# Two alternating running sums in place of one chain in the softmax sums of a graph-attention kernel

## Chip, cores, metric

One core of one Trainium2 chip runs the whole kernel. The metric is device time in microseconds (us), the median of several runs; lower is better. Engines are called as in the profile: PE is TensorE (matmuls), PEld its weight loads, DVE is VectorE, ACT is ScalarE, POOL is GpSimd, SP issues most DMAs.

## The reference, cut to what matters

Two layers on x of shape (16, 1024, 256), each with a layer norm and a relu ahead of it and a residual around it. Layer 0 builds a weight matrix per batch, from it the queries, and then runs softmax attention with four heads of 64 channels; layer 1 is a graph convolution with two linear layers and batch norms. What the change touches is the softmax:

```python
c_adj = jnp.mean(fea, axis=1)
diff = c_adj[:, None, :] - c_adj[:, :, None]
A = jnp.abs(jnp.abs(jax.nn.sigmoid(diff) - 0.5) - 0.5) * 2.0
...
Wg = adj[None, :, :] * A_s
g = jnp.einsum('bcn,bnm->bcm', fea, Wg)
...
attn = jax.nn.softmax(jnp.einsum('bhnd,bhmd->bhnm', q, k) * scale, axis=-1)
out = jnp.einsum('bhnm,bhmd->bhnd', attn, v)
```

## The kernel before, in words

Everything is fp32. The order of the work on every engine is written out by hand (a manual schedule): each engine executes its instructions in the order in which the Python code issues them, and only waits on semaphores are put in between. So "ahead" and "behind" below are places in an engine's queue.

**The loop.** One pass per batch b of 16. It runs the attention of batch b (`attention`, line 732), then the graph of batch b+1 (`graph` at line 385 for b+1 = 1, `graph_seven` at line 501 for the 14 batches from 2 to 15), then the first linear layer of batch b (`linear1_all`). After the loop an output stage does the second linear layer and the residual. A pass through the middle of the loop takes some 131 us.

**The attention** has four steps, two halves g of the queries times two pairs of heads. In a step, `scores` (line 737) loops over eight blocks m of 128 keys. For each, PE makes two 128x512 blocks of scores into one PSUM tile f_s (line 743, three buffers), ACT takes the exponential of the tile into an SBUF tile f_p (line 751, eight buffers), and DVE adds it to a running sum f_acc: block 1 to block 0 at line 757, blocks 2 to 7 into the sum in place at line 760. The sum over the eight tiles is still spread over 128 keys. `partial` (line 764) finishes it: a DVE transpose in 32x32 blocks from f_acc into f_sums (line 768; f_sums is in pool `ow`, one buffer) and a DVE reduction into f_red (line 776). `values` (line 778) multiplies the exponentials by v on PE (line 784) into one PSUM tile f_o, which DVE transposes into f_oT (line 797). PE does scores and values of a step one after the other, and goes on with the next step's scores.

**Between the steps** stand other pieces:
- `hooks` for steps 0 and 1, issued between `scores` and `partial`: `weights(b+1, c)` for c = 0 and 1. That is `differences` (line 350), two ACT operations that make a 128x1024 weight tile f_w from a row of means f_row (absolute value at line 353, tanh at line 356), and `masked` (line 359), one DVE operation that multiplies it by the adjacency tile (line 361). f_row comes by a DMA through DRAM. For b = 0 the hooks also hold column sums of the adjacency on ACT and two small DVE operations; for b = 15 only a relu on ACT.
- the reciprocal of the sums of half 0, in step 2: `collect` (line 807), four ACT copies from f_red to f_parts, is issued inside `scores` after block 5; `invert` (line 814), four DVE operations on f_rec, f_most and f_least (lines 817 to 820), and `spread`, four ACT copies to f_recs (line 826), stand between `scores` and `partial`; `scale` (line 835), one DVE multiplication of f_oT and 16 DMAs on SP, follows `partial`.

**The graph** of the next batch follows on PE right behind the last values. Eight weight tiles c of 128 rows go into it. Tiles 0 and 1 are used plainly (`plain`, matmuls at line 514); tiles 2 to 7 go in three pairs n through a scheme with seven products instead of eight. Its DVE work is a list written out from line 606 on: maskings of tiles 2 to 7 (line 361), the reciprocal of half 1 (lines 817 to 820), differences of halves of the tiles (`make_t1` to `make_t4`, lines 557 to 569, some of them in place in f_w), and the scaling of half 1 (line 835). The matmuls of the pairs are at line 576. PE's list near the end of the maskings is m1(1), m2(1), m4(0), m_7(1), m3(1), m1(2), m2(2), m6(0), m6(1); m1(2) reads tile 6 and m2(2) tile 7.

Of the kernel before, what the change touches and what calls it, by code (L numbers as in the profile page):

```python
# [10 lines left out]
F32 = mybir.dt.float32  # L11
# [6 lines left out]
P = 128  # L18
# [11 lines left out]
def fast_path(  # L30
# [20 lines left out]
    nc = tc.nc  # L51
# [48 lines left out]
    class BatchNorm:  # L100
# [11 lines left out]
        def invert(self, f0, f1, triples=None):  # L112
            for f in range(f0, f1):
                nc.vector.bn_aggr(
                    self.mv[:, f, :],
                    self.st[:, f, :, :].rearrange("p t s -> p (t s)")
                    if triples is None
                    else triples,
                )
            at = slice(f0, f1)  # L120
            nc.vector.tensor_scalar_add(self.var[:, at], self.mv[:, at, 1], EPS)
            nc.gpsimd.tensor_tensor(
                self.rstd[:, at], self.var[:, at], mhalf[:, : f1 - f0], ALU.pow
            )
            if self.offset is not None:
                mean = self.mv[:, at, 0]
                nc.vector.tensor_add(mean, mean, self.offset[:, at])
                nc.vector.tensor_sub(mean, self.offset[:, at], mean)
# [47 lines left out]
    with ExitStack() as stage:  # L176
# [5 lines left out]
        ow = stage.enter_context(tc.tile_pool(name="fow", bufs=1))  # L182
# [15 lines left out]
        for c in range(NC):  # L198
            if LASTING[c] is None:
                t = big.tile([P, N], F32, tag=f"adj{c}", name=f"f_adj_{c}")  # L200
            else:
                t = lasting.tile(
                    [P, N], F32, tag=LASTING[c], name=f"f_adj_{c}", bufs=4 if c < 4 else 1
                )
# [527 lines left out]
        def attention(b, qT, kT, v, hooks):  # L732

            steps = [(g, pair) for g in range(NH) for pair in range(HEADS // 2)]
            p_of, acc_of, oT_of, o_of, red_of = {}, {}, {}, {}, {}

            def scores(s, within=None):
                g, pair = steps[s]
                for m in range(NC):
                    ps = ps_s.tile([P, 2, 512], F32, tag="s", name=f"f_s_{b}_{s}_{m}")  # L740
                    for e in range(2):
                        rows_e = slice(e * HD, (e + 1) * HD)
                        nc.tensor.matmul(  # L743
                            ps[:, e, :],
                            kT[rows_e, pair, ts(m, P)],
                            qT[rows_e, pair, ts(g, 512)],
                            start=True,
                            stop=True,
                        )
                    p = pp.tile([P, 2, 512], F32, tag="p", name=f"f_p_{b}_{s}_{m}")  # L750
                    nc.scalar.activation(p, ps, AF.Exp)  # L751
                    p_of[s, m] = p
                    if m == 1:
                        acc = pp.tile(
                            [P, 2, 512], F32, tag="acc", name=f"f_acc_{b}_{s}", bufs=2
                        )
                        nc.vector.tensor_add(acc, p_of[s, 0], p)  # L757
                        acc_of[s] = acc
                    elif m > 1:
                        nc.vector.tensor_add(acc_of[s], acc_of[s], p)  # L760
                    if m == 5 and within:
                        within()

            def partial(s):

                g, pair = steps[s]
                t = ow.tile([P, 2, 16, 32], F32, tag="sums", name=f"f_sums_{b}_{s}")
                nc.vector.transpose(
                    t.rearrange("p e j i -> p (e j i)"),
                    acc_of.pop(s).rearrange("p e q -> p (e q)"),  # L770
                )
                if pair == 0:
                    red_of[g] = small.tile(
                        [P, HEADS // 2, 2, 16], F32, tag="red", name=f"f_red_{b}_{g}", bufs=1
                    )
                nc.vector.tensor_reduce(red_of[g][:, pair], t, AX.X, ALU.add)  # L776

            def values(s):
                g, pair = steps[s]
                o_of[s] = ps_o.tile([P, 512], F32, tag="o", name=f"f_o_{b}_{s}")  # L780
                for m in range(NC):
                    p = p_of.pop((s, m))
                    for e in range(2):
                        nc.tensor.matmul(  # L784
                            o_of[s][e * HD : (e + 1) * HD, :],
                            v[:, m, ts(2 * pair + e, HD)],
                            p[:, e, :],
                            start=(m == 0),
                            stop=(m == NC - 1),
                        )  # L790
                if pair == 0:
                    oT_of[g] = ow.tile(
                        [P, HEADS // 2, 4, 4, 32], F32, tag="oT", name=f"f_oT_{b}_{g}", bufs=2
                    )


                nc.vector.transpose(
                    oT_of[g][:, pair].rearrange("p j c i -> p c j i"),
                    o_of.pop(s).rearrange("p (c j i) -> p c j i", c=4, j=4),
                )  # L800
# [65 lines left out]
            first = finish(0)  # L866
            collect, invert, spread, scale, add = first
            for i in range(len(steps)):
                scores(i, collect if i == 2 else None)
                for step in hooks.get(i, ()):  # L870
                    step()
                if i == 2:
                    invert()
                    spread()
                partial(i)
                if i == 2:
                    scale()
                values(i)
# [419 lines left out]
        with tc.manual_schedule(engines={ENG.PE, ENG.Activation, ENG.DVE, ENG.Pool, ENG.SP}):  # L1298
# [73 lines left out]
            for b in range(B):  # L1372

                hooks = {}
# [7 lines left out]
                else:  # L1382
                    hooks[0] = [lambda norm=norm: norm.relu(4, NC, False)]
                    w2n = lasting.tile([P, CC, F1], F32, tag="w2n", name="f_w2n")
                    nc.sync.dma_start(w2n, W2.rearrange("(c p) f -> p c f", p=P))
                left = attention(b, *qkv, hooks)

                def more(c):
# [102 lines left out]
    with ExitStack() as stage:  # L1491
# [21 lines left out]
        with tc.manual_schedule(engines={ENG.PE, ENG.Activation, ENG.DVE, ENG.Pool, ENG.SP}):  # L1513
# [31 lines left out]
            sums = lasting.tile([P, 4, 2, P], F32, tag="w2n", name="f_w2s")  # L1545
# [825 lines left out]
```

## Time and profile before

| | |
|---|---|
| median of 3 runs | 2397.92 us (2396.44 to 2398.54) |
| profiled execution: span | 2396.9 us, in 24478 instructions |
| the span beside the median | 1.0 us shorter |
| granted PE clock, mean | 0.995 (1.00 until 2330 us, 0.83 in the last 67 us) |
| DVE adds at line 760 | 384, 470.5 us busy, 1225 ns each |
| DVE adds at line 757 | 64, 76.3 us busy, 1192 ns on the page |
| DVE maskings at line 361 | 127, 152.7 us busy, 1212 ns each |
| ACT exponentials at line 751 | 512, 477.4 us busy, 1048 ns each |
| PE scores, line 743, and values, line 784 | 457.1 and 453.6 us busy |

The page says how busy each engine is over the whole span. The timeline lists the instructions of one engine in order of time; neighbours of one kind are merged into a row with a count, and the first number is the start, the second the time from the first start to the last end. A remark in brackets gives the engine's idle time ahead of the row and what ended it. The records of DVE, ACT and PE instructions overlap their neighbours by some tens of ns[...]; so the distance from start to start tells what an instruction costs its queue, and the duration does not.

Busy time by stretch of one pass, PE, DVE and ACT: attention of batch 8 (1117 to 1175 us) 58.0, 55.3 and 42.4 of 58; the graph up to its last masking (1175 to 1191) 15.8, 15.8 and 9.8 of 16; the rest of the graph (1191 to 1219) 28.0, 22.6 and 11.0 of 28; the linear layer (1219 to 1250) 31.0, 20.4 and 10.9 of 31.

### The profile page before, as it was taken

The numbers are of one execution on the slowest core, as the hardware profiler recorded it, in microseconds if no ns is written. First come the engines' busy times: TensorE is split into PE (matmuls) and PEld (weight loads), VectorE is DVE, ScalarE is ACT, GpSimd is POOL, SyncE is SP. The second block draws the span as 40 slices with busy tenths as digits, with TensorE's granted clock in tenths as the row PEclk, the third lists the DMA queues.
The fourth block names the chain that finished last, engine by engine and source line by source line (L and its number), as shares of the span: only waits on it lengthen the run. The fifth ranks groups of instructions, "written<-read, shape, count | busy, mean of one in ns | idle before, by whom it ended". The sixth has DMA issues, their size and how long they took to land.

```text
span 2396.9 us, 24478 instructions
## 1 busy us (share of the span) xinstructions
PE 2353.8 (98%) x7950; PEld 1032.4 (43%) x7950; DVE 1974.2 (82%) x2806; ACT 1346.8 (56%) x1974; POOL 174.1 (7%) x253
## 2 busy tenths in 40 slices
PE   8999999999999999999999999999999999999995
PEld 4443444434343434444343434344443434444444
DVE  6888889797979798897979797988979798757766
ACT  6845555564736455555647374555555565346654
POOL 2030010101010000101010100001010100000000
PEclk9999999999999999999999999999999999999998
DMA  5042433433342434334323414243433321355569
GB/s 189 8 143 93 144 116 123 136 117 91 98 156 64 160 93 160 100 123 136 120 96 111 140 61 164 87 167 93 137 123 121 115 85 53 114 208 181 174 243 371
DMA packets 178650, 312.44 MB, mean 130 GB/s; under 512 B 33617, under 2 KB 117073, under 8 KB 178513
## 3 DMA queue, kind: packets, MB, share of 16 engines
q1 hardware_dynamic: 164176, 267.25, 33.2%
q0 software_dynamic: 9728, 26.76, 3.7%
q10 hardware_dynamic: 4608, 16.78, 1.7%
q8 instruction: 65, 1.06, 0.2%
q14 instruction: 73, 0.59, 0.1%
HBM read 195.04 MB, written 96.79 MB: 122 GB/s over the span
## 4 chain that ended last, share of the span: by engine, by line
PE 72%; DVE 18%; ACT 4%; issue 3%; DMA 1%; SPq 1%; DVEq 0%; ACTq 0%; POOLq 0%; POOL 0%
PE f_aps L944 16%; PE f_s L743 12%; PE f_o L784 11%; PE f_zps L1050 6%; DVE f_acc L760 6%; PE f_vps L450 5%; PE f_zx L1588 4%; DVE f_w L361 4%; PE f_gpsx L576 3%; PE f_zm L1588 3%; ACT f_p L751 3%; PE f_gps L576 3%; PE f_kpsx L691 2%; PE f_gps L404 2%; PE f_kps L691 2%
## 5 line engine op out<-in xcount | busy, mean ns | idle before, releaser
L751 ACT ACTIVATE f_p<-f_s 128x1024 f32<-128x1024 f32 x512 | 477.4, 1048 | 163.0 <-PE f_s L743 163.0
L760 DVE TENSOR_TENSOR f_acc<-f_acc,f_p 128x1024 f32<-128x1024 f32 x384 | 470.5, 1225 | 41.4 <-DVE f_acc L760 1.4
L743 PE MATMUL f_s<-f_qT,f_kT 64*128 64x512 f32 x2048 | 457.1, 596 | 0.0
L784 PE MATMUL f_o<-f_p,f_v 128*64 128x512 f32 x2048 | 453.6, 595 | 0.0
L743 PEld LDWEIGHTS f_s<-f_qT,f_kT 64*128 64x128 f32 x2048 | 190.2, 185 | 264.4 <-ACT f_p L751 118.6
L784 PEld LDWEIGHTS f_o<-f_p,f_v 128*64 128x64 f32 x2048 | 141.4, 137 | 304.4 <-issue 251.3
L353 ACT ACTIVATE f_w<-f_row,f_col 128x1024 f32<-128x1024 f32 x127 | 147.0, 1157 | 31.6 <-PE f_gps L514 16.8
L361 DVE SCALAR_TENSOR_TENSOR f_w<-f_w,f_adj 128x1024 f32<-128x1024 f32 x127 | 152.7, 1212 | 4.2 <-ACT f_w L356 4.2
L260 POOL TENSOR_TENSOR f_rstd_b<-f_var_b,f_mhalf 128x4 f32<-128x4 f32 (+1 forms) x31 | 33.1, 1069 | 1502.3 <-DVE f_var_b L259 1502.3
L356 ACT ACTIVATE f_w<-f_w 128x1024 f32<-128x1024 f32 x127 | 134.3, 1058 | 4.0
L944 PE MATMUL f_aps<-f_ahatT,f_hs 128*128 128x512 f32 x256 | 115.1, 592 | 0.0
L944 PE MATMUL f_aps<-f_ahatT,f_h_b 128*128 128x512 f32 x256 | 113.4, 596 | 0.0
L450 PE MATMUL f_vps<-f_kvw,f_hT 128*128 128x256 f32 x512 | 113.1, 379 | 0.0
L944 PE MATMUL f_aps<-f_t,f_hs 128*128 128x512 f32 x256 | 112.5, 592 | 0.0
L281 ACT ACTIVATE f_h_b<-f_x,f_shift_b,f_rstd_b 128x256 f32<-128x256 f32 x128 | 66.3, 593 | 75.7 <-DVE f_shift_b L266 75.7
L450 PEld LDWEIGHTS f_vps<-f_kvw,f_hT 128*128 128x128 f32 x512 | 97.3, 190 | 20.1 <-issue 7.4
L281 ACT ACTIVATE f_h_a<-f_x,f_shift_a,f_rstd_a 128x256 f32<-128x256 f32 x126 | 73.8, 587 | 50.5 <-DVE f_shift_a L266 50.5
L514 PE MATMUL f_gps<-f_w,f_h_a 128*128 128x512 f32 x224 | 99.9, 599 | 0.0
L757 DVE TENSOR_TENSOR f_acc<-f_p,f_p 128x1024 f32<-128x1024 f32 x64 | 76.3, 1192 | 14.4 <-ACT f_p L751 14.4
L576 PE MATMUL f_gps<-f_w,f_h_a 128*128 128x512 f32 x168 | 82.7, 601 | 3.8 <-DVE f_w L361 3.8
L1073 ACT ACTIVATE f_z<-f_zps,f_b 128x512 f32<-128x512 f32 x60 | 38.0, 683 | 75.3 <-PE f_zps L1050 75.3
L776 DVE TENSOR_REDUCE f_red<-f_sums 128x32 f32<-128x1024 f32 x64 | 78.1, 1220 | 2.2
(275 smaller groups left out, 3410.6 us busy)
## 6 DMA issues: line engine op xcount, KB each, us to landing
f_t<-ft SPq DMA_DIRECT2D x84, 512.0 KB, 10.9
fz<-f_z SPq DMA_DIRECT2D x64, 512.0 KB, 9.6
f_x<-in_x_dram SPq DMA_DIRECT2D x31, 1024.0 KB, 6.3
f_zb<-fz SPq DMA_DIRECT2D x42, 512.0 KB, 4.2
f_att<-f_oT SPq DMA_DIRECT2D x512, 32.0 KB, 1.9
fx<-f_x SPq DMA_DIRECT2D x16, 1024.0 KB, 4.4
fhT<-f_hQ POOLq DMA_DIRECT2D x112, 128.0 KB, 2.9
f_hT<-fhT SPq DMA_DIRECT2D x28, 512.0 KB, 6.0
```

Source lines behind the costliest of these rows:

```text
L281: nc.scalar.activation(self.h[:, c, :], self.xt[:, c, :], AF.Relu, bias=self.shift[:, c : c + 1], scale=self.rstd[:, c : c + 1], accum_out ...
L353: nc.scalar.activation(w, rows[b], AF.Abs, bias=cols[b][:, c : c + 1], scale=0.5 / C)
L361: nc.vector.scalar_tensor_tensor(w, w, 1.0, adj_t[c], ALU.subtract, ALU.mult)
L450: nc.tensor.matmul(ps[:, i, :], hT[e][:, ts(c4 + i, P)], kvw_t[:, e, C : 2 * C], start=(e == 0), stop=(e == CC - 1),)
L576: nc.tensor.matmul(ps, left, right, start=fresh and n == 0, stop=(n == PAIRS - 1), skip_group_check=more,)
L743: nc.tensor.matmul(ps[:, e, :], kT[rows_e, pair, ts(m, P)], qT[rows_e, pair, ts(g, 512)], start=True, stop=True,)
L751: nc.scalar.activation(p, ps, AF.Exp)
L760: nc.vector.tensor_add(acc_of[s], acc_of[s], p)
L784: nc.tensor.matmul(o_of[s][e * HD : (e + 1) * HD, :], v[:, m, ts(2 * pair + e, HD)], p[:, e, :], start=(m == 0), stop=(m == NC - 1),)
L944: nc.tensor.matmul(ps, left[:, m, :], right(m), start=not more and m == 0, stop=(m == KH - 1), skip_group_check=more,)
L1050: nc.tensor.matmul(ps[i], left[:, ts(i, P)], right, start=not more, stop=True, skip_group_check=more,)
L1588: nc.tensor.matmul(ps, left[:, m, :], right[:, m, :], start=start and m == 0, stop=(m == 1), skip_group_check=not start,)
```

## The change

The running sum is split. Block 1 still starts f_acc from blocks 0 and 1. Block 2 is not added alone any more: at block 3, a second sum starts in the f_sums tile, from blocks 2 and 3. From then on even blocks (4 and 6) are added to f_acc, odd blocks (5 and 7) to f_sums. One more add joins f_sums into f_acc; there are seven adds in a step, as before. The join is issued at the end of `scores`, behind the steps that used to stand between `scores` and `partial`: the hooks (with the weight tile's masking) and, in step 2, `invert` and `spread`. The transpose in `partial` then writes into the same f_sums tile that held the second sum, so that tile is taken at block 3 of a step and not at its end.

```diff
-            p_of, acc_of, oT_of, o_of, red_of = {}, {}, {}, {}, {}
-
-            def scores(s, within=None):
+            p_of, acc_of, odd_of, oT_of, o_of, red_of = {}, {}, {}, {}, {}, {}
+
+            def scores(s, within=None, before_last=()):
...
                         acc_of[s] = acc
-                    elif m > 1:
-                        nc.vector.tensor_add(acc_of[s], acc_of[s], p)
+                    elif m == 3:
+                        odd = ow.tile([P, 2, 16, 32], F32, tag="sums", name=f"f_sums_{b}_{s}")
+                        odd_of[s] = odd
+                        flat = odd.rearrange("p e j i -> p e (j i)")
+                        nc.vector.tensor_add(flat, p_of[s, 2], p)
+                    elif m > 3:
+                        to = flat if m % 2 else acc_of[s]
+                        nc.vector.tensor_add(to, to, p)
                     if m == 5 and within:
                         within()
+                for step in before_last:
+                    step()
+                nc.vector.tensor_add(acc_of[s], acc_of[s], flat)
 
             def partial(s):
...
-                t = ow.tile([P, 2, 16, 32], F32, tag="sums", name=f"f_sums_{b}_{s}")
+                t = odd_of.pop(s)
...
             for i in range(len(steps)):
-                scores(i, collect if i == 2 else None)
-                for step in hooks.get(i, ()):
-                    step()
-                if i == 2:
-                    invert()
-                    spread()
+                scores(
+                    i,
+                    collect if i == 2 else None,
+                    [*hooks.get(i, ()), *([invert, spread] if i == 2 else [])],
+                )
                 partial(i)
```

## Prediction

> **What bounds the kernel now.** I read the page first, then TensorE's own waits, then the timeline of one batch on TensorE and on VectorE (DVE), and last the start times of all 7950 matmuls.
>
> ```profile
> PE 2353.8 (98%) x7950; PEld 1032.4 (43%) x7950; DVE 1974.2 (82%) x2806; ACT 1346.8 (56%) x1974; POOL 174.1 (7%) x253
> ```
>
> TensorE is busy 98% of 2396.9 us, so little can be won. What can, is its waiting. Of the waits of TensorE on another engine, those at the start (9.7 us on the adj load) and in the output stage (line 1811), and three under 1 us, lie outside the code that is changed. One is left:
>
> ```profile
> PE f_gps L576 <- DVE f_w L361: 3.8, 14, 0.6
> ```
>
> It comes 14 times, once in each batch that goes through the seven-product graph. In TensorE's timeline of one batch (columns: start us, us, engine, line, operation, tiles, count):
>
> ```profile
> 1188.72 1.02 PE L576 MATMUL f_gps<-f_w,f_gs 128*128 128x512 f32 x2
> 1189.58 1.02 PE L576 MATMUL f_gpsx<-f_w,f_h_a 128*128 128x512 f32 x2
> 1190.80 1.12 PE L576 MATMUL f_gps<-f_w,f_h_a 128*128 128x512 f32 x2 [0.20 <-DVE f_w L361]
> ```
>
> Pairs start 0.86 us apart (0.429 a matmul), so the third pair was due at 1190.44 and came at 1190.80: 0.36 late. It takes 1.12 where others take 1.02: the second matmul is 0.10 late too. The wait of 0.20 in brackets is less than the loss because matmul records overlap. It is matmul m2(2), which reads weight tile 7, and that tile was masked just then. On DVE, from the last attention step on:
>
> ```profile
> 1164.64 1.18 DVE L757 TENSOR_TENSOR f_acc<-f_p,f_p 128x1024 f32<-128x1024 f32 x1
> 1165.93 7.88 DVE L760 TENSOR_TENSOR f_acc<-f_acc,f_p 128x1024 f32<-128x1024 f32 x6
> 1173.84 1.25 DVE L768 STREAM_TRANSPOSE f_sums<-f_acc 128x1024 f32<-128x1024 f32 x1
> 1175.12 1.22 DVE L776 TENSOR_REDUCE f_red<-f_sums 128x32 f32<-128x1024 f32 x1
> ...
> 1188.39 1.22 DVE L835 TENSOR_TENSOR f_oT<-f_oT,f_recs 128x1024 f32<-128x1024 f32 x1
> 1189.53 1.22 DVE L361 SCALAR_TENSOR_TENSOR f_w<-f_w,f_adj 128x1024 f32<-128x1024 f32 x1
> ```
>
> No row between 1123.6 and 1194 shows idle time ahead of it: DVE works without a break from the first add of the attention until past tile 7, which ends at 1189.53 + 1.22 = 1190.75, and TensorE goes on 0.05 later. So DVE sets this stall. In three batches one add is 0.36 us slower than its like, and there the stall is 0.72 and not 0.36: a delay of DVE within the attention reaches TensorE whole.
>
> The adds themselves: six of line 760 take 7.88 us, less one duration of 1.225 that is 6.65 for five steps: 1.33 us from add to add, though one lasts 1.225. Each reads what the one before wrote. Compare instructions that do not read their forerunner:
>
> ```profile
> 1132.69 1.22 DVE L361 SCALAR_TENSOR_TENSOR f_w<-f_w,f_adj 128x1024 f32<-128x1024 f32 x1
> 1133.83 1.24 DVE L768 STREAM_TRANSPOSE f_sums<-f_acc 128x1024 f32<-128x1024 f32 x1
> ```
>
> The masking starts 1.14 us before the next one, of the same length. That transpose does wait for a DVE result, the add's, but one that is an instruction old. So a wait for the latest result costs 1.33 - 1.14 = 0.19 us, and for an older one nothing.
>
> **What the Trainium skill says.** "VectorE: DVE Perf Modes", section "The TRN2 errata": an fp32 tensor_tensor takes (N+151)/0.96 ns, 1224 at N = 1024; the trace has 1225. The same page, section "The DRAIN you can't avoid": a next op does not start until the pipe is empty, and semaphores between chained ops cost nothing. The trace differs: 1.14 against 1.33, and the measurement decides. "Perfetto Trace Analysis", section "Identifying the Most-Contended Engine": matmul busy time is no measure of headroom, being pipelined; the trace agrees (0.20 shown, 0.46 lost), hence my start-to-start distances.
>
> **The change part by part.** All times of a step count from the start of its first exponential; exponential m ends at 1.03 + 0.907 m.
>
> *The adds.* Seven before, seven after, all 128x1024. Before: first to second 1.29, then 5 x 1.33, then 1.26 to the transpose: 9.20 us in the last step (1164.64 to 1173.84). After: m = 1, 3, 4, 5, 6, 7, where each reads a sum two instructions old: 5 x 1.14 = 5.7; then the join, which reads add 7 in the last step, 1.33, and 1.26 to the transpose: 8.3. That is 0.9 less.
>
> *What ScalarE leaves of it.* Add 3 needs the fourth exponential, at 3.75. In the steps the first add starts at 3.87, 3.06, 2.23 and 2.60 before. I replay DVE's queue with these numbers (the replay of the old order gives 3.03, 2.20, 2.58 for the latter three and the last transpose at 11.78 against a measured 11.80). After: step 0 saves up to 1.0, but its masking, due at 10.7, waits for tanh, which ends at 9.6 to 11.5; step 1 starts its first add at 2.0 to 2.9 and waits for exponentials; step 2 starts at 1.97, at ScalarE's pace, and loses more since exponentials 6 and 7 come 1.09 later there, behind four copies. Step 3 starts at 2.44 instead of 2.58, its add 3 at 3.80, its transpose at 10.9 instead of 11.8. So steps 0 to 2 give back nearly all they save, and 0.87 us is left at the end.
>
> *The moved steps.* Masking (hooks of steps 0 and 1), the four reciprocal operations and the four copies of step 2 now stand ahead of the join. ScalarE's order stays; no DMA is issued by them, so SP's and POOL's queues are passed by nothing. Behind the masking's wait stand join, transpose, reduction and output transpose; who waits for these is the next step's copies and the output buffer of TensorE, needed at about 20 in a step and free at 16. The join behind the masking is free of the 0.19; the transpose behind it no longer is: 0.12, counted above. The odd sum takes its buffer five adds earlier than the transpose did; its last reader, the reduction of the step before, is over by then.
>
> *From DVE to TensorE.* After the last output transpose DVE stays busy to tile 7. Would another wait eat the 0.87? Tanh of tiles 5, 6 and 7 ends at 1180.87, 1184.30 and 1186.43, their maskings start at 1183.59, 1185.93 and 1189.53: 0.87 earlier still fits, by 0.76 at the closest. The in-place difference at 1184.72 must follow a matmul that ends at 1183.74: 0.11 to spare. So tile 7 ends 0.87 earlier; 0.36 is enough in 11 batches, 0.72 in three. The surplus buys nothing, since TensorE is then back to back.
>
> *The sum.* The excess distance ahead of m2(2), over all 14 batches by start times, is 6.0 us; the second matmul's 0.10 makes 1.4 more. 7.4 us go. What is late next: nothing that waits on DVE; TensorE's distances are 0.429 but for about 0.1 at each change between scores and values, present with DVE early or late. The loads for the rest of the batch are issued from freed buffers and move along. Span 2396.9 - 7.4 = 2389.5; the median of the runs lies 1.0 above this span, so 2390.5, -0.31%.
>
> **Unknown costs.** The new adds into another tile: no row; between 1.18 (line 757, into a fresh tile) and 1.23 (line 760) long, I take 1.14 start to start. If the second matmul's 0.10 belongs to the change of tiles and stays, the gain is 6.0: 2391.9. Below: the output stage runs at a granted clock of 0.83[...]; three runs differ by 2.1 us, so 1 to 2 us either way.
>
> **Rivals.**
> - *The pipe holds every add.* If an add cannot start before the last one is out, whatever it reads, as the skill says, the adds after m = 3 keep 1.33. Then step 2 ends 0.25 later (transpose behind the join), and the last transpose comes at 11.9 instead of 11.8: 14 x 0.1 = 1.4 us more, 2399.3, within 0.2%. Against it: 1.14 ahead of the transpose behind the masking. Chance 0.10.
> - *Half of it comes through.* A wait not seen now takes over at tile 7 (the in-place difference with its 0.11, or ScalarE's copies), and half the stall stays: 2394.2. For it: several margins are tenths of a us. Chance 0.09.
> - *Slower: the masking's wait now holds the join.* In step 0 join, transpose, reduction and output transpose stand behind a masking that waits for the row's DMA and tanh. By the replay the last transpose is later than 11.8 only when tanh of step 0 ends after 14.6; the latest seen is 11.5. If the row came so late, each us beyond costs 14 us; 0.5 us gives 2405. For it: this row is already waited for, 1.4 us in this batch; against it: 3.1 us of slack. Chance 0.04.
>
> **Chances and range.** My forecast has 0.77. A measurement of this kernel can tell about 0.2%, 4.8 us, from no change. Faster by more than that: the forecast, and a share of the half case, 0.80; within: 0.16; slower 0.04. The range goes from 2388.5 (7.4 and 2 us of the output stage) to 2394.5, which takes in the half case.
>
> **What would show it.** Right: adds 3 to 7 at 1.14 apart where DVE is behind; the last transpose 8.3 after its first add; tile 7 masked about 0.9 earlier against the matmul ahead; no wait of line 576 on line 361; matmul distances of 0.429 there. Wrong: adds still 1.33 apart (first rival), a new releaser of that matmul (second), idle DVE ahead of the masking in step 0 that grows past 14.6 (third).

## The result and the profile after

| | before | after |
|---|---|---|
| median of 8 runs each | 2397.95 us (2396.43 to 2399.53) | 2391.53 us (2390.04 to 2392.53) |
| profiled execution | span 2396.9 us | own time 2392.53 us, span 2390.7 us |
| DVE busy | 1974.2 us | 1953.6 us |
| PE's share of the chain that ended last | 72%, DVE 18% | 97%, DVE 1% |

The ratio is 0.9974, with a 95% interval from 0.9964 to 0.9984: 6.4 us, or 0.27%, faster. The median of the runs stands 0.8 us above the profiled span, where it stood 1.0 above it before.

The page of the kernel after, busy time of each engine (us, share of the span, instructions):

```profile
PE 2351.4 (98%) x7950; PEld 1032.3 (43%) x7950; DVE 1953.6 (82%) x2806; ACT 1345.3 (56%) x1974; POOL 174.9 (7%) x253
```

The same page, the chain that ended last, by engine:

```profile
PE 97%; DMA 1%; DVE 1%; issue 0%; ACT 0%; SPq 0%; DVEq 0%; ACTq 0%; POOLq 0%; POOL 0%
```

TensorE's busy time is all but unchanged (2353.8 to 2351.4), and the counts of working instructions are the same. DVE's busy time falls by 20.6 us because its records overlap more: overlapping records are counted once. The chain, which went through DVE for 18% of the span, now hardly leaves TensorE. Those 18% say which way the chain ran, and not what DVE cost: TensorE lost 7.5 us to it in all. The wait of line 576 on line 361 (14 times before) is not in the list of TensorE's waits any more. TensorE's timeline of batch 8, the same products as those shown of before (start, length, count at the end):

```profile
1186.93 1.02 PE L576 MATMUL f_gpsx<-f_w,f_h_a 128*128 128x512 f32 x2
1187.79 1.02 PE L576 MATMUL f_gps<-f_w,f_h_a 128*128 128x512 f32 x2
1188.65 1.96 PE L576 MATMUL f_gpsx<-f_kT,f_gs 128*128 128x512 f32 x4
```

The pair that reads tile 7 (second row) comes 0.86 after the one ahead and takes 1.02: no stall. (A matmul's record here is 0.59 long and the next starts 0.43 later, so TensorE's records overlap by 0.16, more than the tens of ns said above.) The row after it is 1.96 long; four matmuls without a gap take 1.88. I come back to those 0.08.

DVE's timeline of the same batch, last attention step and then tile 7:

```profile
1161.82 1.18 DVE L757 TENSOR_TENSOR f_acc<-f_p,f_p 128x1024 f32<-128x1024 f32 x1
1163.19 1.22 DVE L763 TENSOR_TENSOR f_sums<-f_p,f_p 128x1024 f32<-128x1024 f32 x1 [0.19 <-ACT f_p L751]
1164.34 1.22 DVE L766 TENSOR_TENSOR f_acc<-f_acc,f_p 128x1024 f32<-128x1024 f32 x1
1165.47 1.22 DVE L766 TENSOR_TENSOR f_sums<-f_sums,f_p 128x1024 f32<-128x1024 f32 x1
1166.61 1.22 DVE L766 TENSOR_TENSOR f_acc<-f_acc,f_p 128x1024 f32<-128x1024 f32 x1
1167.74 1.22 DVE L766 TENSOR_TENSOR f_sums<-f_sums,f_p 128x1024 f32<-128x1024 f32 x1
1168.99 1.22 DVE L771 TENSOR_TENSOR f_acc<-f_acc,f_sums 128x1024 f32<-128x1024 f32 x1
1170.25 1.25 DVE L777 STREAM_TRANSPOSE f_sums<-f_acc 128x1024 f32<-128x1024 f32 x1
...
1185.94 1.22 DVE L361 SCALAR_TENSOR_TENSOR f_w<-f_w,f_adj 128x1024 f32<-128x1024 f32 x1
```

An add still lasts 1.22, but add follows add after 1.13 to 1.15. The join starts 1.25 after the add whose result it reads, the transpose 1.26 after the join. From first add to transpose it is 8.43 us, before 9.20. Tile 7 is ready at 1185.94 + 1.22 = 1187.16, and the matmul that reads it starts at 1187.79. Over the 14 batches the median is 0.64 us ahead of time, before it was 0.30 behind.

**Where the time went.** I split the span by the start of each batch's attention. From the first one to the last, after is 6.35 us shorter: 0.38 or 0.39 in a batch, 0.73 to 0.75 in the three that had a delayed add. For line 576's matmuls I take what each distance from start to start has beyond 0.429 and add that up over the 14 batches; this is called the excess below. It gives the same number by another way: 7.53 us before, 1.18 after, so 6.35 less. Ahead of the first attention, after is 0.77 us longer (TensorE waits there for the adjacency load), and from the start of the last one on, 0.67 shorter; batch 15's attention, which has the change in it, takes TensorE the same time to 0.01 us, and the 0.67 arise in the output stage behind it. I put neither down to the change: in the kernel with one chain through two tiles (below), which gains nothing, these two stretches are 0.72 longer and 1.60 shorter than before. 0.77 - 6.35 - 0.67 = -6.25, the difference of the spans but for rounding.

**Where the savings of the first three steps went.** Groups by line of the kernel after (busy us, mean ns, then the engine's idle time ahead of them and what ended it):

```profile
L763 DVE TENSOR_TENSOR f_sums<-f_p,f_p 128x1024 f32<-128x1024 f32 x64 | 78.3, 1223 | 21.8 <-ACT f_p L751 21.8
L757 DVE TENSOR_TENSOR f_acc<-f_p,f_p 128x1024 f32<-128x1024 f32 x64 | 76.8, 1200 | 28.4 <-ACT f_p L751 28.4
```

The same view of the kernel before:

```profile
L757 DVE TENSOR_TENSOR f_acc<-f_p,f_p 128x1024 f32<-128x1024 f32 x64 | 76.3, 1192 | 14.4 <-ACT f_p L751 14.4
```

Before, the first add of a step (line 757) had 14.4 us of idle time ahead of it. Now it has 28.4, and the first add of the second sum 21.8 more: DVE runs into the exponentials and waits for them. That is slack in the middle of a batch, and not time.

### The profile page after: what moved, and what is told of

It is laid out like the page before. It is cut to its first block, busy times and chain, and to the rows that moved or that the text cites. A ratio compares the mean times of both kernels' runs of the same rounds, so it can differ in the third digit from the quotient of the medians.

```text
span 2390.7 us, 24368 instructions
## 1 busy us (share of the span) xinstructions
PE 2351.4 (98%) x7950; PEld 1032.3 (43%) x7950; DVE 1953.6 (82%) x2806; ACT 1345.3 (56%) x1974; POOL 174.9 (7%) x253
## 4 chain that ended last, share of the span: by engine, by line
PE 97%; DMA 1%; DVE 1%; issue 0%; ACT 0%; SPq 0%; DVEq 0%; ACTq 0%; POOLq 0%; POOL 0%
PE f_s L743 19%; PE f_o L793 19%; PE f_aps L952 16%; PE f_zps L1058 6%; PE f_gps L576 6%; PE f_vps L450 5%; PE f_gpsx L576 5%; PE f_gps L514 4%; PE f_zx L1596 4%; PE f_zm L1596 3%; PE f_kpsx L691 2%; PE f_gps L404 2%; PE f_kps L691 2%; PE f_z2ps L1534 1%; PE f_outps L1819 1%; PE f_zps L1140 1%
## 5 line engine op out<-in xcount | busy, mean ns | idle before, releaser
L766 DVE TENSOR_TENSOR f_acc<-f_acc,f_p 128x1024 f32<-128x1024 f32 x128 | 155.9, 1218 | 4.2 <-ACT f_p L751 4.2
L766 DVE TENSOR_TENSOR f_sums<-f_sums,f_p 128x1024 f32<-128x1024 f32 x128 | 155.8, 1217 | 0.0
L757 DVE TENSOR_TENSOR f_acc<-f_p,f_p 128x1024 f32<-128x1024 f32 x64 | 76.8, 1200 | 28.4 <-ACT f_p L751 28.4
L514 PE MATMUL f_gps<-f_w,f_h_a 128*128 128x512 f32 x224 | 99.9, 599 | 0.0
L763 DVE TENSOR_TENSOR f_sums<-f_p,f_p 128x1024 f32<-128x1024 f32 x64 | 78.3, 1223 | 21.8 <-ACT f_p L751 21.8
L777 DVE STREAM_TRANSPOSE f_sums<-f_acc 128x1024 f32<-128x1024 f32 x64 | 79.7, 1245 | 2.2
```

The lines of the kernel that those rows point to most:

```text
L514: nc.tensor.matmul(gps[d][:, ts(g, 512)], h[:, c, ts(d, P)], w[:, ts(g, 512)], start=(c == 0), stop=(c == PLAIN - 1),)
L766: nc.vector.tensor_add(to, to, p)
```

## Experiments

The theory: all of the gain is the last step's adds, which no longer wait for their forerunner's result; the last transpose comes 0.9 us earlier, tile 7 with it, and TensorE's one DVE stall goes. Rivals: the gain comes from the other three steps; it comes from the order of the join and the masking; it comes from writing two tiles by turns, whatever the adds read; the tile 7 stall was no cause but a symptom. Every experiment was timed beside the kernel before, and is compared with after by its trace.

### The two sums in the last step alone

```diff
+                    elif not (s == 3):
+                        if m > 1:
+                            nc.vector.tensor_add(acc_of[s], acc_of[s], p)
                     elif m == 3:
...
-                nc.vector.tensor_add(acc_of[s], acc_of[s], flat)
+                if s == 3:
+                    nc.vector.tensor_add(acc_of[s], acc_of[s], flat)
...
```

> Two sums in step 3 only; steps 0 to 2 keep the chain of seven adds. My theory: what steps 0 to 2 save is given back at ScalarE's pace, so nearly the whole gain of the change stays: 2391.5 us, the last transpose 8.4 us after the step's first add, no wait of line 576 on a masking. Rival (each step's saving adds up at the end): a quarter of the gain, some 2396.4 us.

Measured: 2392.28 us (2391.72 to 2394.48), ratio 0.9976 [0.9966, 0.9986]. DVE's timeline of batch 8 in this kernel:

```profile
1161.75 1.18 DVE L757 TENSOR_TENSOR f_acc<-f_p,f_p 128x1024 f32<-128x1024 f32 x1
...
1168.75 1.23 DVE L775 TENSOR_TENSOR f_acc<-f_acc,f_sums 128x1024 f32<-128x1024 f32 x1
1170.01 1.25 DVE L785 STREAM_TRANSPOSE f_sums<-f_acc 128x1024 f32<-128x1024 f32 x1
```

First add to transpose takes 8.26: here the last step starts later, so the fourth exponential is there and the 0.19 us of waiting of after is gone. Either way the transpose comes 10.86 after the step's first exponential, as in after (11.80 before). The excess of line 576 is 1.18, and the stretch from the first to the last attention 6.40 shorter than before. So the last step carries the whole gain of the loop. What the other three steps add is slack: in five batches (1, 4, 7, 10 and 13) a chained add of step 0 is 0.36 late, and tile 7 is 0.38 to 0.43 ahead of time; in after, where the traces show no such late add, it is 0.61 to 0.64 ahead in every batch.

### The two sums in the first three steps alone

The same edit with the other condition:

```diff
+                    elif not (s < 3):
...
+                if s < 3:
+                    nc.vector.tensor_add(acc_of[s], acc_of[s], flat)
...
```

> The mirror image: two sums in steps 0 to 2, the chain in step 3. My theory: step 3 starts some 0.17 us earlier than in the kernel before and then takes the old 9.2 us, so m2(2) still waits, about 0.19 instead of 0.36: 2395 us, between 2394.5 and 2396. Rival (savings add up): three quarters of the gain, 2393.1 us.

Measured: 2393.98 us (2392.56 to 2396.24), ratio 0.9982 [0.9976, 0.9989]: 4.1 us of 6.4, more than I gave it. DVE's timeline of batch 8 in this kernel:

```profile
1162.96 1.18 DVE L757 TENSOR_TENSOR f_acc<-f_p,f_p 128x1024 f32<-128x1024 f32 x1
1164.24 7.87 DVE L761 TENSOR_TENSOR f_acc<-f_acc,f_p 128x1024 f32<-128x1024 f32 x6
1172.15 1.25 DVE L785 STREAM_TRANSPOSE f_sums<-f_acc 128x1024 f32<-128x1024 f32 x1
```

The last step takes 9.19, the old length, but starts 2.42 after its first exponential and not 2.60, so its transpose comes 0.19 earlier. That is what my replay gave (2.44). In an ordinary batch, tile 7 is still too late, by less, and 0.19 us are saved. My range was wrong on the three batches with a delayed add: 0.55 is saved in each, because the delayed add, which stood in the chain of step 0 or 2 before, does not occur in the two sums that now stand there. One batch (2) has a new delayed add in its last step, which is still a chain, and loses 0.16. In all, the excess falls from 7.53 to 3.98. So the rival's 2393.1 was nearer to the number, but by another way than its own: the first three steps' gain reaches the end only as an earlier start of the last step and as delays that do not occur. The two parts don't add up (6.40 and 3.55 against 6.35 together), since both go against the same stall, and the last step alone is enough to end it.

### The join ahead of the masking

```diff
+                nc.vector.tensor_add(acc_of[s], acc_of[s], flat)
                 for step in before_last:
                     step()
-                nc.vector.tensor_add(acc_of[s], acc_of[s], flat)
```

> Two sums in all steps, but the join stands ahead of the hooks and of the reciprocal, as the last add did before the change. My theory: the place of the join is worth under 0.1 us in steps 0 to 2, which is given back to ScalarE's pace, and nothing in step 3, where nothing stands between: 2391.5 us. Rival (the join hidden behind the masking is what pays): most of the gain gone, 2396 us or more.

Measured: 2391.03 us (2390.35 to 2391.99), ratio 0.997 [0.9959, 0.9981]; line 576's excess is 1.18. The transposes of the first three steps come at 13.07, 11.88 and 12.40 where after has 13.06, 11.97 and 12.39. In after, behind the masking, the join no longer follows the add whose result it reads, but the transpose follows the join. With the join ahead of the masking it is the other way round. The wait only changes its place, and the runs show no difference.

### One chain through two tiles

Six adds by turns into f_sums and f_acc, each still reading the result of the one ahead, and no join.

```diff
...
-                    elif m > 3:
-                        to = flat if m % 2 else acc_of[s]
-                        nc.vector.tensor_add(to, to, p)
+                    elif m > 1:
...
+                        to, of = (acc_of[s], flat) if m % 2 else (flat, acc_of[s])
+                        nc.vector.tensor_add(to, of, p)
...
-                nc.vector.tensor_add(acc_of[s], acc_of[s], flat)
```

> One chain of seven adds that writes in turn into the two tiles: no add is in place, but each still reads the newest sum. My theory: the 0.19 us is the wait for the newest result, so adds stay 1.33 apart and the time is that of the kernel before, 2398 us. Rival (adding in place is what costs): adds 1.14 apart and 2391.5 us.

Measured: 2397.8 us (2397.02 to 2398.48), ratio 0.9998 [0.9989, 1.0006]. DVE's timeline:

```profile
1166.53 1.23 DVE L765 TENSOR_TENSOR f_sums<-f_acc,f_p 128x1024 f32<-128x1024 f32 x1
1167.86 1.23 DVE L765 TENSOR_TENSOR f_acc<-f_sums,f_p 128x1024 f32<-128x1024 f32 x1
```

TensorE's waits in the same kernel:

```profile
PE f_gps L576 <- DVE f_w L361: 3.5, 13, 0.5
```

No add writes where it reads, and they are still 1.33 apart; the stall is back, with an excess of 7.35. So it is not the write in place, nor the use of two tiles, but the dependence on the add just ahead that makes 0.19 us. This kernel does not tell reading from overwriting, since each add reads the newest sum and also overwrites a tile that the add ahead has read. DVE's timeline of before holds a pair that does:

```profile
1185.33 0.69 DVE L557 TENSOR_TENSOR f_kT<-f_w,f_w 128x512 f32<-128x512 f32 x1
1185.93 1.22 DVE L361 SCALAR_TENSOR_TENSOR f_w<-f_w,f_adj 128x1024 f32<-128x1024 f32 x1
...
1190.78 0.69 DVE L557 TENSOR_TENSOR f_v<-f_w,f_w 128x512 f32<-128x512 f32 x1
1191.51 0.69 DVE L561 TENSOR_TENSOR f_w<-f_w 128x512 f32<-128x512 f32 x1
```

Line 561 reads nothing that line 557 wrote; it only overwrites a half tile that line 557 read. It starts 0.71 to 0.73 us behind it in all 28 places where they are neighbours, and the masking, which touches none of line 557's tiles, 0.60. So a wait for the instruction just ahead costs its tenth of a us for an overwritten operand too.

### An idle operation ahead of the maskings: 0.40 and 1.00 us

A DVE reduction over 320 or 896 columns of an adjacency tile, whose result nobody reads, in the list of the seven-product graph.

```diff
...
+            nc.vector.tensor_reduce(idle, adj_t[2][:, 0:320], AX.X, ALU.add)
             masked(b, 2)
```

> The changed kernel with one idle DVE reduction of 320 columns (0.40 us of DVE's queue, its result is not used) between the last output transpose and the masking of tile 2, in the 14 batches. My theory: in the changed kernel the masking of tile 7 ends 0.64 us before its matmul is due, and some 0.58 of that is to spare, so 0.40 costs nothing: 2391.5 us. Rival (DVE's time reaches TensorE whole from the first ns): 14 x 0.40 = 5.6 us more, 2397 us.

> The same with 896 columns, 1.00 us of DVE's queue, its result not used. My theory: 1.00 less 0.58 to spare leaves 0.42, and 0.10 for the second record of m2(2), less the 0.08 that m6(0) waits for ScalarE in the changed kernel, makes 0.44 a batch: 6 us more, 2397.6 us, with the wait of line 576 on the masking back. Rival (the gain has another cause than DVE's lead at tile 7): 2391.5 us, no such wait.

Measured with 0.40: 2391.38 us (2389.73 to 2391.62), ratio 0.9969 [0.9958, 0.998]; tile 7 is 0.24 ahead of time, and no wait on it is listed. With 1.00: 2397.09 us (2396.28 to 2398.97), ratio 0.9996 [0.9988, 1.0005]. TensorE's timeline in the kernel with 1.00:

```profile
1189.55 1.02 PE L577 MATMUL f_gpsx<-f_w,f_h_a 128*128 128x512 f32 x2
1190.82 1.13 PE L577 MATMUL f_gps<-f_w,f_h_a 128*128 128x512 f32 x2 [0.25 <-DVE f_w L362]
```

The pair comes 1.27 after the one ahead, 0.41 more than 0.86, and the excess of all batches is 7.23, or 6.05 more than in after. 0.64 of slack less 0.40 is 0.24, and less 1.00 it is 0.36 late (the matmul starts 0.05 after tile 7 is done): the slack is real, and beyond it DVE's delay reaches TensorE in full. That is the stall of before, put back without touching a single add, so tile 7's time is the cause and no symptom.

### Another product between the copy and m6(0)

What is left in after are 0.084 us per batch, in the row of 1.96 above. TensorE's weight loads in after, same stretch:

```profile
1187.80 0.19 PEld L576 LDWEIGHTS f_gps<-f_w,f_h_a 128*128 128x128 f32 x1 [0.24 <-issue]
1188.63 0.30 PEld L576 LDWEIGHTS f_gpsx<-f_kT,f_gs 128*128 128x128 f32 x2 [0.65 <-ACT f_v L641]
```

ScalarE's timeline of after:

```profile
1187.99 0.58 ACT L641 COPY f_v<-f_gpsx 128x512 f32<-128x512 f32 x1 [4.21 <-PE f_gpsx L576]
```

m1(2) ends the sum in f_gpsx, ACT copies it out until 1188.57, and only then may m6(0) add to it. Loads come one matmul ahead when nothing holds them (0.19 each, 0.43 apart); here the first is held, and two come together at 1188.63, 0.30 in all. The first matmul is on time, the second 0.084 late. In before the load of m2(2) looks the same, two in 0.30 at 1190.80, and that is its second matmul's 0.10:

```profile
1190.80 0.30 PEld L576 LDWEIGHTS f_gps<-f_w,f_h_a 128*128 128x128 f32 x2 [1.03 <-DVE f_w L361]
```

There m6(0) lost nothing, and its loads came one by one: m2(2) was 0.46 us late, and the copy was done. If that is so, a product in between takes it away:

```diff
             m2(2)
+            m_7(2)
             m6(0)
             m6(1)
             make_t4(1)
             make_t4(2)
-            m_7(2)
```

> The changed kernel with the matmul m_7(2) moved ahead of m6(0) on TensorE, so that ScalarE's copy of x has one more matmul to finish under. My theory: the distance of 0.513 between the two records of m6(0) falls to 0.429, 0.084 x 14 = 1.2 us: 2390.3 us, which is the part of my forecast that did not come. Rival (that excess is the change of tiles in PSUM and not a wait for the copy): the 0.08 stays or moves to the next pair, 2391.5 us.

Measured: 2389.5 us (2389.22 to 2390.42), ratio 0.9964 [0.995, 0.9977]. TensorE's timeline in this kernel:

```profile
1187.52 1.02 PE L576 MATMUL f_gps<-f_w,f_h_a 128*128 128x512 f32 x2
1188.38 1.02 PE L576 MATMUL f_gps<-f_v,f_kt 128*128 128x512 f32 x2
1189.23 1.88 PE L576 MATMUL f_gpsx<-f_kT,f_gs 128*128 128x512 f32 x4
```

1.88 and not 1.96, m6(0)'s weights are loaded one by one again (0.19 each, 0.43 apart), and the excess is 0.00 in all 14 batches. From the first to the last attention it is 7.45 us shorter than before, 1.10 more than after. This is the fastest kernel of the study; its last 0.9 us against after's 2391.53 lie outside this stretch, where the runs vary.

### A later tanh in the first step

Nine small copies on ACT, whose result nobody reads, ahead of the weight tile of step 0, to try the slower rival's point.

```diff
+                if i == 0 and 0 < b < B - 1:
+                    late = [lambda: nc.scalar.copy(idle, ones)] * 9
...
-                    [*hooks.get(i, ()), *([invert, spread] if i == 2 else [])],
+                    [*late, *hooks.get(i, ()), *([invert, spread] if i == 2 else [])],
```

> The changed kernel with nine idle ScalarE copies of 128x32 (their result is not used) ahead of the first weight tile's two operations in step 0 of 14 batches, so that its masking, and the join behind it, wait some 2.7 us longer: tanh ends near 13.5 us after the step's first exponential instead of 10.7. My theory: steps 1 to 3 take up the delay at ScalarE's pace, since the limit lies at 14.6: step 3 begins at 2.42 as before, 2391.5 us. Rival (the join held by the masking is passed on): up to 14 x 2 us more, clearly over 2398 us.

Measured: 2391.07 us (2390.47 to 2391.62), ratio 0.997 [0.9959, 0.9982]. The dose came out too small. The nine copies took 2.29 us, 0.25 each, and tanh ended at 11.7, not 13.5 as I had meant. DVE's timeline of batch 8 in this kernel, the masking of step 0:

```profile
1127.79 1.22 DVE L362 SCALAR_TENSOR_TENSOR f_w<-f_w,f_adj 128x1024 f32<-128x1024 f32 x1 [0.95 <-ACT f_w L357]
```

The masking waits 0.95 us and holds the join behind it. Step 1 starts at 3.06 and not at 2.04, step 2 at 1.97 again, and nothing is lost. This confirms that the wait holds the join and that a step absorbs it, but not the point of 14.6. The larger dose came by itself. In batch 7 of after, the store of the row of means to DRAM landed 13.9 us after its issue (978.30 to 992.20; the median of the 14 stores is 9.9), and DVE's timeline there shows:

```profile
999.80 1.22 DVE L361 SCALAR_TENSOR_TENSOR f_w<-f_w,f_adj 128x1024 f32<-128x1024 f32 x1 [2.79 <-ACT f_w L356]
```

2.79 us of waiting, tanh's end at 13.5; the steps start at 4.90, 3.03 and 2.42, and the last one is on time. Put into my replay, that tanh gives 4.86, 3.03 and 2.41. A tanh past 14.6 was seen in no run, so the loss beyond it stays an extrapolation.

### The join first and the product first; the changed kernel again

Both edits from above in one kernel, and the changed kernel unchanged, to see what one more run of it gives.

> Both orders together: the join ahead of the hooks, and m_7(2) ahead of m6(0). My theory: the first is worth nothing, the second 1.2 us: as the kernel with the second alone, 2389.5 to 2390.3 us. Rival (both pay): some 2389 us.

> The changed kernel once more, beside the other two on the same chip. My theory: 2391.5 us again, 1 to 2 us above the kernel with m_7(2) first. Rival (the difference between these two is the spread between chips): the two within 0.3 us.

Measured: 2389.95 us (2389.62 to 2390.68), ratio 0.9966 [0.9954, 0.9978], excess 0.00, for the first; 2391.51 us (2390.01 to 2391.78), ratio 0.9972 [0.9961, 0.9982], excess 1.17, for the second. The join's place brings nothing here either. The changed kernel repeats to 0.02 us, with another late row in batch 7 (step 1 at 4.70) and the same 2.42 in step 3. Both kernels of this pair ran on one chip and stand 1.6 us apart, so the gain of the moved product is not a difference between chips.

## Why the prediction was right, and where its sum was off

- **The bound.** Right. The one DVE stall of TensorE in the changed code was the wait of m2(2) for tile 7; it is gone, and putting DVE back by 1.00 us brings it back.
- **The price of an add.** Right: 1.13 to 1.15 from start to start, predicted 1.14. The rival that the pipe holds every add is refuted. "VectorE: DVE Perf Modes", section "The DRAIN you can't avoid", from which it came, also says that an op which is not held starts earlier, and the 1.13 agree with that. It also says, of a row of eight copies, that a semaphore behind each cost nothing. The prediction took that for waits as well, which is more than it says. In these traces every add signals a semaphore, at 1.13 as at 1.33, so the signal is free here too; what costs is to wait for the newest one, 0.19 us on 1.14, and a wait for one that is an instruction older costs nothing. The one-chain kernel through two tiles shows that the dependence makes the difference.
- **The join.** I took 1.33, like an add on the sum ahead; it is 1.25. Those 0.08 account, to the hundredths of the replay, for tile 7 coming 0.94 earlier and not 0.87. The traces show one difference between the two. A chained add waits for two engines, ScalarE and DVE itself, and the wait for DVE is an instruction of its own in DVE's queue, 384 of them at line 760, 21 ns each. The join, like the transpose, waits for DVE alone and has no such instruction. In batch 8 of before the separate wait starts 0.04 us after the add ahead has ended, and its add 0.07 later; in after the join starts 0.04 after the end of the add that it reads. So of the 0.19, some 0.12 go with the wait for the newest result and 0.07 with its being a separate instruction. No experiment took that instruction away.
- **The replay of the queue.** Right in what it was for. Step 3 starts at 2.42, its transpose comes at 10.86 (predicted 10.9), and steps 0 to 2 give their savings back at ScalarE's pace. What it left out is the delayed adds, which are gone where two sums stand; that showed in the experiment on the first three steps.
- **The sum: this is the step that failed, in size.** Predicted were 7.4 us in the loop, 6.0 of pitch and 1.4 for the second matmul's 0.10; measured are 6.35. "What is late next: nothing that waits on DVE" holds by the letter, but I asked only about DVE. Next was ScalarE: with m2(2) on time, m6(0) is due before the copy of f_gpsx is over, and the 1.4 us move two products down, where 1.18 of them stay. My second unknown, that the 0.10 might stay (then 6.0, 2391.9), was the right number for a wrong reason: it belongs to a held pair of weight loads and not to a change of tiles. The kernel with m_7(2) moved gets those 1.1 us.
- **The median.** 2391.53 against 2390.5: 1.1 from that term; what moved at the start (+0.77) and in the output stage (-0.67) cancelled.
- **The rivals.** Half coming through did not occur: the in-place difference and the tanhs were in time, as the slack of 0.64 and its test with 0.40 show. The slower one's mechanism is real, and its slack was enough for the latest tanh of these runs, 13.5, which is later than the 11.5 I had to judge by.

**What stays open.** Why single adds come 0.36 us late; where they do is told in the last section. Why the adjacency load and the output stage move by 0.7 us each. No experiment was on either.

## What to carry to other kernels

Price an engine's dependent chain by start-to-start distances in the trace, not by durations: two alternating sums hid a wait of 0.19 us per add at the same number of instructions (0.12 where the wait was not a separate instruction), and it paid only in the one step whose end TensorE waits for. When you take a stall away, ask of every engine, not only of the one that made it, what the stall had been hiding: here a copy on ScalarE that had been done in time only because the matmul ahead was late. A moved independent product then gave what was left.

## What I had not expected of the hardware

- A weight load that is held takes the next one with it: two in 0.30 us where they are otherwise 0.43 apart, and the second matmul is late by 0.08 to 0.10 though the first is on time. So a wait that ends just in time for a matmul still costs.
- A chained DVE add is now and then 0.36 us late, and not at random. In before its separate wait starts on time, but the add follows 0.42 us later and not 0.07. Counted from the first record of DVE, waits included, the late adds are numbers 960, 1216, 2496 and 3264; the kernel with one chain through two tiles has the same four; with two sums in the last step alone they are 320, 960, 1600, 2240 and 2880, and with two sums in the first three steps, 576. All are multiples of 64. These four kernels have 1213 instructions behind a separate wait that was still open when the instruction ahead ended. Of them 22 fall on a multiple of 64, and 14 of these are late; of the 1191 others none is. In after only 15 such instructions are left, none on a multiple of 64, and no add is late. Why a 64th is late, and why eight were not, the traces do not show.
- The same small DMA store takes 8.8 to 13.9 us from issue to landing (median 9.9). The latest is that of batch 7, and step 1 of that batch starts nearly as late when the kernel is run again (4.70). Tanh of step 0 ends latest in batch 7 in the kernel before too (11.5).
